# Reordering the end of layer 0 and the last scan step of a four-layer convolution and state-space kernel

## The chip, the cores and the metric

The kernel runs on one core of a Trainium2 chip. The metric is the device time of one execution in microseconds. The kernel before was timed three times: 3322.79, 3324.20 and 3326.24 us, median 3324.2 us. One more execution was profiled; times inside it count from the start of its span.

Names used below: PE is the matrix engine (PEld its weight loads), DVE the vector engine, ACT the scalar engine, POOL the GpSimd engine, SP the engine that only issues transfers. All data are 32-bit floats.

## The reference, cut to what matters

The input x has 3 images of 256 channels and 48 x 48 pixels. Four layers follow one another, each as x = x + layer(group_norm(x)):

- Layer 0: a 1x1 convolution with SiLU gives y1 and y2; y2 passes two blocks of attention and MLP, in which the three images are query, key and value of each other; then y1, y2 and the two block results are concatenated and go through a 1x1 convolution with SiLU.
- Layer 1: a 3x3 convolution whose weights differ by image. Eight experts' weights are mixed with a routing vector made from the image's channel means:

```
pooled = x.mean(axis=(2, 3))
routing = jax.nn.sigmoid(pooled @ routing_ws)
ws = jnp.einsum('ne,eoihw->noihw', routing, weight)
```

- Layer 2: a 3x3 convolution with one set of weights and a bias.
- Layer 3: a state-space layer. Per image it runs a recurrence over 2304 tokens for 512 channels with 16 states each, `hst = hst * dA + dt * B * u`, and reads out `y = sum over states of hst * C`, then gates with silu(z) and projects back to 256 channels.

## The kernel before, in words

The image index b runs in the order ORDER = (2, 1, 0) almost everywhere, and the 2304 pixels are cut into six chunks of 384.

**End of layer 0** (lines 1002 to 1102). For each image two loops of six chunks follow each other. In the first, the MLP of the second block: `hidden` (line 513) makes two products and two gelus, `add_back` (line 526) makes two accumulated products in PSUM tile acc, of which there are three, and DVE adds them to cur[b] (line 533). In the second, `concatenated` (line 1027) multiplies the three stored strips yc of a chunk and the chunk of cur[b] with the last weights (line 1031), ACT applies SiLU (line 1036), and POOL adds the input strip xc (line 1041). DVE then takes statistics of the chunk before (line 1045). The strips yc (576 KB) and xc (384 KB) are loaded by `parts` (line 1017) through ACT's queue; three are requested in front of the loops, and then, in chunk number k, those of chunk k + 2. The pool of the strips has three buffers of each.

After the six chunks of an image the generator `routing` (line 359) is put in line. It makes the group norm of the new image, the channel means and the routing vector. Each call of `aside` (line 1054) advances it to its next yield. Its last piece broadcasts the pooled means on DVE (pbc, line 373, one buffer), multiplies them with the routing weights on PE (line 374), for both halves of the channels, and ends with a sigmoid on ACT (line 378).

**Expert mixing.** `mixed(2, ...)` (line 265) is another generator, for the first image of layer 1. It has 48 steps of one 128x768 piece of an expert's weights (8 experts x 2 channel halves x 3 taps); each piece is loaded by SP into one of six buffers wconv (line 251). The six steps of the first expert run on ACT (line 294), the other 42 on DVE (line 296, an accumulation in u). Two more steps then make `kernel_transform` (line 254), one for each channel half: six DVE operations, lines 258 to 263, from the three mixed taps to six transformed ones, with one wconv buffer for an intermediate. `aside(n)` advances the mixing n steps, from the moment that route[2] exists: 2 in each MLP chunk, 3 in each concatenation chunk.

**Input transform.** Layer 1 is a Winograd-like convolution: `input_transform` (line 316) pads and scales half an image with two ACT operations (line 331) and three POOL fills (lines 322, 325) into the tile xpad, which has one buffer, and makes six transformed inputs vt with twelve DVE operations (lines 345 to 356). For the first half of image 2 it is called in chunk 3 of the last image's concatenation. `products` (line 1623) multiplies vt with u on PE (line 1627); `output` (line 1635) adds the products into x on DVE (lines 1645 to 1657). Five PSUM tiles hold products. While the convolution of image 2 runs, image 1's weights are mixed beside it.

**Order of the work.** `keep_order` (line 2120) chains the instructions of PE, DVE, ACT and POOL, each in the order in which they were written, from a mark to the place of its call. It covers the two loops at the end of layer 0 up to the rest of the mixing (line 1096), and the whole of layer 3 (there with SP too). What is written in between, the routing of image 0 and layers 1 and 2, is not chained; a planner sorts it by its own estimate of when operands are there, and may set such an instruction between two chained ones.

**Last step of layer 3** (lines 2007 to 2115). A step is a chunk, a channel group m and a half h of the states; it has eight scans on DVE (line 1942), one after the other, whose decays ACT makes ahead (line 1934). There are 144 steps; `end` is the last. After a step POOL multiplies its states with C (`times_c`, line 1950), and `add_states` (line 1969) sums the products of the step before over the states: PE multiplies them with a folding matrix into y_ps (line 1964). `keep_busy` (line 1367) issues products that nobody reads, called fillers, into the spare columns of the PSUM tile ps_r (line 1370). In the last step C is copied to that PSUM tile (line 2019) and the products with C are made in three pieces on DVE (`last_product`, line 1983), each followed by its sums. The fillers and the sums stand there so:

```
                n = busy.get((m, h, part), 0)
                if (s == 0 and 2 <= part <= 5) or (s == end and 4 <= part <= 6):
                    n = 3
...
            if s >= 1:
                add_states(s - 1)
```

The fillers of part 4 to 6 are written after `last_product((0,), (2, 3))` of part 5 or around it; the sums of step end - 1 are written after the last scan. Then follow the last sums, the gate (line 1993), four products (line 1407), two copies and the store (lines 1417, 1418).

Of the kernel before, what the change touches and what calls it, by code (L numbers as in the profile page):

```python
# [84 lines left out]
def net(  # L85
# [273 lines left out]
    def routing(b, psum, tag, stats):  # L359

        mv, sc, sh = yield from group_norm_steps(b, psum, tag, stats)
        norms[b] = sixth(sc, sh)
        pooled = small.tile([P, CT], F32, name="pooled")
        nc.vector.tensor_tensor(pooled, mv[:, :, 0], sc, ALU.mult)
        nc.vector.tensor_tensor(pooled, pooled, sh, ALU.add)
        yield
        pr = psum.tile([P, 512], F32, tag=tag, name="ps_r")  # L370
        for ct in range(CT):
            pbc = small.tile([P, P], F32, name="pbc", bufs=1)
            nc.vector.tensor_scalar(pbc, ones, pooled[:, ct : ct + 1], None, ALU.mult)
            nc.tensor.matmul(
                pr[:, :EXPERTS], pbc, rwt[:, ct, :], start=ct == 0, stop=ct == CT - 1
            )
        r = route[b] = const.tile([P, EXPERTS], F32, name=f"route{b}")
        nc.scalar.activation(r, pr[:, :EXPERTS], AF.Sigmoid)


    with ExitStack() as l0:
# [36 lines left out]
        with ExitStack() as p1:  # L418
# [15 lines left out]
            for b in ORDER:  # L434
                xb = xin.tile([P, CT, N], F32, name="xb")

                parts = 6 if b == ORDER[0] else 1
# [576 lines left out]

        def parts(b, c):

            yc = ypool.tile([P, 3, CH], F32, name="yc")
            nc.scalar.dma_start(yc, ycat[b][:, :, c * CH : (c + 1) * CH])  # L1020
            xc = ypool.tile([P, CT, CH], F32, name="xc")
            nc.scalar.dma_start(
                xc, x[b, :, c * CH : (c + 1) * CH].rearrange("(t p) n -> p t n", p=P)
            )
            return yc, xc

        def concatenated(b, c, yc, xc):
            pz = pair()
# [18 lines left out]
        i = NB - 1  # L1047
        mark = listed[-1]
        chunks = [(b, c) for b in ORDER for c in range(NCH)]
        ahead = [parts(*chunks[z]) for z in range(3)]  # L1050
        small_steps = [mlp_weights(i, 0)]
        mixing = mixed(2, upools[0])

# [11 lines left out]
        for n, b in enumerate(ORDER):  # L1065
            held = None
            for c in range(NCH):
                f = hidden(b, c)
                if held is not None:
                    add_back(i, *held)  # L1070
                held = b, c, f
                aside(2)
            add_back(i, *held)
            stats = [
                small.tile([P, NCH, 6], F32, name=f"xst{m}", bufs=2) for m in range(CT)
            ]
            for c in range(NCH):
                concatenated(b, c, *ahead.pop(0))

                z = n * NCH + c + 2  # L1080
                if 3 <= z < len(chunks):
                    ahead.append(parts(*chunks[z]))
                if c:
                    take_stats(b, c - 1, stats)
                if b == 0 and c == 3:
                    vp = late_pool("vp", 2, last_pools)
                    pad = late_pool("pad", stack=last_pools)
                    first_v = input_transform(2, 0, *norms[2])
                aside(3)
            take_stats(b, NCH - 1, stats)  # L1090
            if b:
                curpools[b].close()
            small_steps.append(routing(b, psm, "m", stats))
# [14 lines left out]
    rooms, w3v, chunks, stored = {}, {}, {}, set()  # L1108
# [699 lines left out]
    with ExitStack() as l3:  # L1808
# [198 lines left out]
        for s, (at, m, h) in enumerate(steps):  # L2007
            if m == 0 and h == 1 and at + 2 <= last:
                fetch(at + 2)
            for part in range(8):  # L2010
                j = 4 * m + 2 * h + part // 4
                scan(s, part)
                decay(8 * s + part + 3)
                if s == end and part == 0:
                    c_rows = psr.tile([P, 2, 512], F32, name="ps_r")
                    spread_tiles[:] = [c_rows]
                    tiles["c"], tiles["hc"] = c_rows, hcp.tile([P, 2, 4, CH], F32, name="hc")
                    for g in range(2):
                        nc.tensor.matmul(
                            c_rows[:, g, :CH], ident, chunks[at].bc[1][:, 2 * h + g, :],  # L2020
                            start=True, stop=True,
                        )
                if s == end and part == 3:
                    begin_sums(chunks[at], m)
                    last_product((0, 1), (0, 1))
                if s == end and part == 5:
                    last_product((0,), (2, 3))
                n = busy.get((m, h, part), 0)
                if (s == 0 and 2 <= part <= 5) or (s == end and 4 <= part <= 6):
                    n = 3  # L2030
                if n:
                    g, q = parts_of_step[part]
                    keep_busy(tiles[s][:, g, q, 1 : P + 1], n)
                if s == end and part == 0:
                    for mo in range(2):
                        project_y(chunks[at], mo, 0, 2)
                if s == end and part == 2:
                    gate(at, DI - 2)
                    for mo in range(2):
                        project_y(chunks[at], mo, 2, DI - 1)  # L2040
                if s == end - 1 and part == 0:
                    residual(chunks[at])
                if part == 0 and h == 0:
                    c, n = (at, m + 1) if m + 1 < DI else (at + 1, 0)
                    if c <= last:
                        rows = getattr(chunks[c], "rows", {})
                        chunks[c].rows = {**rows, n: spread(chunks[c], n)}
                if part == 0 and h == 1 and s + 1 < len(steps):
                    spread_second(chunks[steps[s + 1][0]], steps[s + 1][1])
                if part == 4 and s + 1 < len(steps):  # L2050
                    first_states(s + 1)
                if s == 0:
                    if part == 0:
                        scanned = next(
                            i for i in reversed(listed) if i.engine == mybir.EngineType.DVE
                        )
                        tc.add_manual_dep(
                            last_write, scanned.name,
                            mybir.DependencyInfo(
                                mybir.DependencyClass.NoSync, mybir.DependencyReason.DATA  # L2060
                            ),
                            reason="order",
                        )
                    if part == 1:
                        fill_upper(1, 0, 1)
                    if part == 0:
                        run(at, j, PE_)
                    if part in (0, 3, 4, 6):
                        next(pending)
                    if part in (0, 2, 4):  # L2070
                        ct, lo, hi, t = late_copies[part // 2]
                        copy_tokens(ct, lo, hi, t)
                    if part == 5:
                        for copied in last_tokens()[2:]:
                            store_copied(*copied)
                if s == 1:
                    if part % 2 == 0:
                        diagonal(part // 2)
                    if part == 1:
                        next(pending)  # L2080
                if part % 4 == 0:
                    run(at, j, BEGIN)
                if part % 4 == 1:
                    run(at, j, MID)
                if part % 4 == 2:
                    run(at, j, DONE)
                if h == 1 and part == 7 and 3 <= s < end:
                    gate(*steps[s - 3][:2])
                if part % 4 == 3:
                    run(at, j, LATE)  # L2090
                if part == 3 and s:
                    run(at, j, PE_)
            if s + 1 < len(steps):
                fill(s + 1)
            if s == 0:
                next(pending)
            last_states(s)
            if s == end:
                last_product((1,), (2, 3), (2, 3))
            else:  # L2100
                times_c(s)
            run(at, 4 * m + 2 * h + 1, PE_)
            if s >= 1:
                add_states(s - 1)

            if h == 0 and s + 2 < len(steps):
                spread_pe(chunks[steps[s + 2][0]], steps[s + 2][1])
# [122 lines left out]
```

## Time and profile before

| What | us |
|---|---|
| runs: lowest, median, highest | 3322.79, 3324.20, 3326.24 |
| the profiled execution, its own time | 3321.43 |
| its span, first to last instruction | 3319.7 |
| PE busy, DVE busy, ACT busy, POOL busy | 3142.7, 2859.8, 2394.6, 1335.6 |
| DVE scans of layer 3 (L1942), 1152 | 1002.3 |
| PE products of layers 1 and 2 (L1627), 1728 | 429.6 |
| mixing step on DVE (L296), each | 0.95 to 1.01, started 0.93 apart |
| first matmul of the concatenation (L1031), last end | 1350.0 to 1495.6 |
| first product of layer 1 (L1627) | 1514.4 |
| first product of the last output (L1407, after the gate) | 3310.7 |

An instruction is named by its line, engine and tiles (result <- operands). "Idle before" is the time that the engine stood still before it, with the instruction or transfer that ended the wait. Matmul ends are modelled, and one multiplication of 32-bit floats stands as two matmuls in the trace. PEclk or "granted clock" is the share of the full PE clock. A DMA share is the mean busy share of the 16 transfer engines.

### The profile page before, as it was taken

How to read it: one execution, taken by the hardware profiler on the slowest of the kernel's cores; microseconds unless marked ns; L12 is line 12 of the kernel's file. 1: busy time of each engine (PE TensorE's matmuls, PEld its weight loads, DVE VectorE, ACT ScalarE, POOL GpSimd, SP SyncE). 2: the span in 40 equal slices, each digit the busy share in tenths (PEclk: the TensorE clock that was granted, in tenths of full speed). 3: DMA queues.
4: the chain of work that ended last, by engine and by line, in shares of the span. 5: the costliest groups of instructions: out<-in, count | busy, mean ns of one | idle time of the engine just before them, and what ended most of it. 6: DMA issues, size and time to landing. Idle time of an engine off the chain costs nothing.

```text
span 3319.7 us, 54251 instructions
## 1 busy us (share of the span) xinstructions
PE 3142.7 (95%) x20936; PEld 1559.1 (47%) x20936; DVE 2859.8 (86%) x3225; ACT 2394.6 (72%) x3676; POOL 1335.6 (40%) x457
## 2 busy tenths in 40 slices
PE   7999999999999999987999998999999999999996
PEld 4334343353343434555777774444444444444442
DVE  3799989968988998269985449999999999999998
ACT  3688888838888887432324458888888888888884
POOL 0000000000000000120000008999999999999997
PEclk9999999999999999998999999999999999999998
DMA  4000000010000001485621025555555555555652
GB/s 170 30 8 10 8 9 7 8 47 5 8 7 8 9 8 33 148 275 171 212 98 42 34 69 137 137 131 129 133 135 142 138 139 132 122 135 141 147 128 56
DMA packets 182656, 290.98 MB, mean 88 GB/s; under 512 B 34849, under 2 KB 148961, under 8 KB 180466
## 3 DMA queue, kind: packets, MB, share of 16 engines
q1 hardware_dynamic: 169426, 268.53, 30.2%
q10 hardware_dynamic: 12960, 18.88, 1.8%
q8 instruction: 166, 2.72, 0.4%
q14 instruction: 104, 0.85, 0.1%
HBM read 236.24 MB, written 50.64 MB: 86 GB/s over the span
## 4 chain that ended last, share of the span: by engine, by line
PE 54%; DVE 29%; ACT 8%; issue 4%; DMA 2%; POOL 1%; SPq 0%; ACTq 0%; DVEq 0%; POOLq 0%
DVE hs L1942 19%; PE ps_s L638 16%; PE acc L651 14%; PE ps_c L1627 7%; DVE hs L1889 3%; ACT ps_da L1934 2%; DVE u L296 2%; PE ps_y L462 2%; PE ps_s L1031 2%; PE ps_m L665 2%; PE ps_m L711 1%; PE acc L529 1%; PE ps_s L518 1%; PE ps_g L1222 1%; DMA wconv<-in_we 1%
## 5 line engine op out<-in xcount | busy, mean ns | idle before, releaser
L642 ACT ACTIVATE pt<-ps_s 128x1024 f32<-128x1024 f32 x972 | 942.4, 1022 | 154.7 <-PE ps_s L638 142.0
L1942 DVE TENSOR_TENSOR_SCAN hs<-ps_da,hs 128x385 f32<-128x385 f32 x1152 | 1002.3, 934 | 6.1 <-ACT ps_da L1934 5.0
L857 DVE TENSOR_TENSOR part<-part,pt 128x2048 f32<-128x2048 f32 x396 | 906.5, 2289 | 41.3 <-ACT pt L642 18.5
L1934 ACT ACTIVATE ps_da<-dtr,u 128x384 f32<-128x384 f32 x1136 | 642.2, 580 | 116.1 <-DVE hs L1942 105.3
L164 POOL TENSOR_TENSOR rstd<-ve,mhalf 128x2 f32<-128x2 f32 (+1 forms) x25 | 15.7, 628 | 1422.8 <-DVE ve L162 1422.8
L638 PE MATMUL ps_s<-q,kt 32*128 32x512 f32 (+1 forms) x4320 | 576.4, 592 | 0.1
L651 PE MATMUL acc<-pt,vt 128*32 128x512 f32 (+1 forms) x4320 | 520.9, 561 | 0.2
L1627 PE MATMUL ps_c<-vt,u 128*128 128x288 f32 x1728 | 429.6, 409 | 21.9 <-DVE u L263 21.9
L1950 POOL TENSOR_TENSOR hc<-hs,x 128x3072 f32<-128x3072 f32 x72 | 405.5, 5632 | 10.2 <-DVE hs L1942 5.5
L1950 POOL TENSOR_TENSOR hc<-hs,bc 128x3072 f32<-128x3072 f32 x71 | 400.1, 5635 | 8.9 <-DVE hs L1942 4.6
L1627 PEld LDWEIGHTS ps_c<-vt,u 128*128 128x128 f32 x1728 | 328.9, 191 | 117.7 <-issue 20.7
L638 PEld LDWEIGHTS ps_s<-q,kt 32*128 32x128 f32 x4320 | 195.2, 183 | 199.1 <-issue 120.2
L651 PEld LDWEIGHTS acc<-pt,vt 128*32 128x32 f32 x4320 | 94.4, 108 | 353.4 <-issue 326.7
L1964 PE MATMUL ps_y<-hc,u 128*32 128x384 f32 x2304 | 223.8, 505 | 2.1 <-POOL hc L1950 1.1
L1908 POOL TENSOR_TENSOR hs<-dtur,bc 128x1536 f32<-128x1536 f32 x72 | 209.7, 2913 | 0.0
L1273 PE MATMUL ps_g<-u 128*128 128x384 f32 x576 | 195.3, 492 | 11.7 <-ACT u L1269 11.7
L1908 POOL TENSOR_TENSOR hs<-dtur,x 128x1536 f32<-128x1536 f32 x70 | 203.7, 2910 | 0.0
L1273 PEld LDWEIGHTS ps_g<-u 128*128 128x128 f32 x576 | 108.4, 191 | 95.0 <-ACT u L1269 22.5
L1643 ACT COPY cb<-ps_c 128x288 f32<-128x288 f32 x48 | 19.1, 399 | 154.2 <-PE ps_c L1627 129.2
L322 POOL MEMSET xpad<- 128x212 f32 x12 | 5.6, 470 | 307.5 <-ACT xpad L1678 227.7
L1964 PEld LDWEIGHTS ps_y<-hc,u 128*32 128x32 f32 x2304 | 61.6, 111 | 140.3 <-issue 126.8
L1392 PE MATMUL ps_g<-u 128*128 128x384 f32 x288 | 109.2, 513 | 13.1 <-ACT sz L1400 7.7
(295 smaller groups left out, 4163.0 us busy)
## 6 DMA issues: line engine op xcount, KB each, us to landing
wconv<-in_we SPq DMA_DIRECT2D x144, 384.0 KB, 4.3
dtr<-dtd SPq DMA_DIRECT2D x284, 192.0 KB, 3.7
dtur<-dtud SPq DMA_DIRECT2D x284, 96.0 KB, 4.2
wconv<-xd SPq DMA_DIRECT2D x36, 384.0 KB, 4.2
x<-bcd SPq DMA_DIRECT2D x72, 192.0 KB, 4.8
dtd<-x SPq DMA_DIRECT2D x36, 384.0 KB, 3.1
bc<-bcd SPq DMA_DIRECT2D x72, 192.0 KB, 4.9
dtuq<-dtud SPq DMA_DIRECT2D x284, 48.0 KB, 2.0
```

Of the source, the lines that this page charges most:

```text
L638: nc.tensor.matmul(s[:, j, cols], kt[r, mt * P : (mt + 1) * P], q[r, :n], start=True, stop=True,)
L642: nc.scalar.activation(p[:, h0 : h0 + 2, :], s, AF.Exp)
L651: nc.tensor.matmul(acc[h * HD : (h + 1) * HD, :n], vt[:, mt, g * P + h * HD : g * P + (h + 1) * HD], p[:, h, cols], start=mt == 0, stop=mt ...
L857: ): nc.vector.tensor_tensor(part, first, p, ALU.add)
L1273: nc.tensor.matmul(bank[m % 2], w3v["taps"][:, m, tap, :], w3v["xi"][:, m % 3, tap : tap + CH], start=tap == 0, stop=tap == DCONV - 1,)
L1392: nc.tensor.matmul(bank[j], w("in", ct * 512 + m * P, P), k.xn[:, ct, DCONV - 1 :], start=ct == 0, stop=ct == CT - 1,)
L1627: nc.tensor.matmul(pc[:, :HN], u[:, i, dy, ct, m * P : (m + 1) * P], vt[:, i, ct, dy * TW : dy * TW + HN], start=ct == 0 and dy == 0, stop ...
L1908: nc.gpsimd.tensor_tensor(states(s)[:, :, 2:4, 1:], chunks[at].rows[m][1].unsqueeze(1).broadcast_to([P, 2, 2, CH]), b_rows(s, 0, 2), ALU.mult,
L1934: nc.scalar.activation(slots[n % 3][:, 1 : CH + 1], chunks[at].rows[m][0][:, q, :], AF.Exp, scale=amat[:, col : col + 1],)
L1942: nc.vector.tensor_tensor_scan(b, slots[(8 * s + part) % 3][:, : CH + 1], b, 0.0, ALU.mult, ALU.add)
L1950: nc.gpsimd.tensor_tensor(hc, tiles[s][:, :, :, 1:], cb.broadcast_to([P, 2, 4, CH]), ALU.mult)
L1964: nc.tensor.matmul(k.y_ps[32 * q : 32 * q + 32, :CH], fold, hc[:, g, q, :], start=False, stop=g == 1 and q in ends,)
```

## The change

Four edits, all of order; no computation is added or left out except for the fillers.

1. In `routing`, for images 1 and 0 a yield is put between each broadcast on DVE and its product on PE, so that the product is issued an aside later. (For image 0 the generator is run at once, so its order stays.)
2. `parts` is split: xc is still requested two chunks ahead, yc now three chunks ahead, and after xc.
3. In the last image, `aside` advances the mixing three steps instead of two in every second MLP chunk, and in chunk 2 of the concatenation it runs the mixing to its end, both kernel transforms included. This is one chunk ahead of the input transform, which stays in chunk 3.
4. In the last step of layer 3 the fillers of parts 4 to 6 go, and the sums of the step before are issued in part 5, behind `last_product((0,), (2, 3))`, instead of after the last scan.

```diff
@@ routing
             nc.vector.tensor_scalar(pbc, ones, pooled[:, ct : ct + 1], None, ALU.mult)
+            if b < 2:
+                yield
             nc.tensor.matmul(
@@
-        def parts(b, c):
-
+        def rows_of(b, c):
             yc = ypool.tile([P, 3, CH], F32, name="yc")
             nc.scalar.dma_start(yc, ycat[b][:, :, c * CH : (c + 1) * CH])
+            return yc
+
+        def tokens_of(b, c):
             xc = ypool.tile([P, CT, CH], F32, name="xc")
             nc.scalar.dma_start(
                 xc, x[b, :, c * CH : (c + 1) * CH].rearrange("(t p) n -> p t n", p=P)
             )
-            return yc, xc
+            return xc
@@
-        ahead = [parts(*chunks[z]) for z in range(3)]
+        ahead = [(rows_of(*chunks[z]), tokens_of(*chunks[z])) for z in range(3)]
+        rows_ahead, tokens_ahead = ([pair[j] for pair in ahead] for j in range(2))
@@
-                aside(2)
+                aside(3 if n == 2 and c % 2 else 2)
@@
-                concatenated(b, c, *ahead.pop(0))
+                concatenated(b, c, rows_ahead.pop(0), tokens_ahead.pop(0))
 
                 z = n * NCH + c + 2
                 if 3 <= z < len(chunks):
-                    ahead.append(parts(*chunks[z]))
+                    tokens_ahead.append(tokens_of(*chunks[z]))
+                if z + 1 < len(chunks):
+                    rows_ahead.append(rows_of(*chunks[z + 1]))
                 if c:
                     take_stats(b, c - 1, stats)
                 if b == 0 and c == 3:
                     vp = late_pool("vp", 2, last_pools)
                     pad = late_pool("pad", stack=last_pools)
                     first_v = input_transform(2, 0, *norms[2])
-                aside(3)
+                aside(3 if n < 2 or c < 2 else 99)
@@
                 if s == end and part == 5:
                     last_product((0,), (2, 3))
+                    add_states(end - 1)
                 n = busy.get((m, h, part), 0)
-                if (s == 0 and 2 <= part <= 5) or (s == end and 4 <= part <= 6):
+                if s == 0 and 2 <= part <= 5:
                     n = 3
@@
             run(at, 4 * m + 2 * h + 1, PE_)
-            if s >= 1:
+            if 1 <= s < end:
                 add_states(s - 1)
```

## The prediction, made before the changed kernel was run

> **What bounds the kernel now.** I first read the page's engine shares. PE is busy 95% of the span and DVE 86%, so anything that shifts by less than a few microseconds can only be found in stretches where PE stops. I then asked for the busy time in stretches around the two places that the diff touches: the end of layer 0 (1402 to 1600 us) and the last step (3290 to 3320 us).
>
> ```profile
> 1402.00:1440.00 38.00, 34.50 (x101) 19.41 (x100) 21.96 (x29) 9.03 (x14) 9.78 (x6) 0.96 0.91 310
> 1440.00:1464.00 24.00, 19.53 (x54) 10.94 (x55) 16.63 (x35) 11.51 (x17) 2.78 (x2) 0.86 0.71 241
> 1464.00:1496.00 32.00, 30.83 (x95) 17.59 (x93) 18.76 (x23) 9.26 (x13) 10.44 (x8) 1.00 0.74 246
> 1496.00:1514.40 18.40, 0.00 (x0) 0.00 (x0) 18.30 (x23) 7.81 (x10) 2.51 (x4) 0.62 0.19 64
> 1514.40:1600.00 85.60, 83.79 (x331) 62.14 (x331) 81.81 (x143) 17.29 (x27) 1.54 (x4) 0.98 0.64 218
> ```
>
> The columns are the stretch, its length, busy us of PE, PEld, DVE, ACT and POOL, granted clock, DMA share, GB/s. The reader is to see the fourth row: for 18.4 us PE does nothing while DVE never rests. The first two rows show PE short by 3.5 and 4.5 us. In the last row PE and DVE are both full, so neither can start layer 1 late without moving the end.
>
> The timeline then says what PE waits for, and what DVE did meanwhile.
>
> ```profile
> 1414.23 3.47 PE L1031 MATMUL ps_s<-yc,w0b 128*128 128x384 f32 x6 [1.92 <-DMA yc<-ycat]
> 1428.03 2.17 PE L1031 MATMUL ps_s<-yc,w0b 128*128 128x384 f32 x6 [1.54 <-DMA yc<-ycat]
> 1453.17 0.59 PE L374 MATMUL ps_r<-rwt,pbc 128*128 128x8 f32 x2 [3.55 <-DVE pbc L373]
> 1489.94 0.81 DVE L345 SCALAR_TENSOR_TENSOR wc<-xpad 128x624 f32<-128x624 f32 x1 [5.67 <-ACT xpad L331]
> 1491.73 2.25 POOL L1041 TENSOR_TENSOR x<-x,xc 128x768 f32<-128x768 f32 x1 [2.67 <-ACT x L1036]
> 1492.23 2.42 DVE L348 TENSOR_TENSOR vt<-wc,we 128x624 f32<-128x624 f32 x1
> 1513.34 0.95 DVE L263 TENSOR_TENSOR u<-wconv,u 128x768 f32<-128x768 f32 x1
> 1514.43 11.18 PE L1627 MATMUL ps_c<-vt,u 128*128 128x288 f32 x38 [18.89 <-DVE u L263]
> ```
>
> In the brackets stand the idle time and what ended it. PE waits twice for a y strip, once for a routing operand behind mixing steps on DVE, and 18.89 us for the kernel transform. DVE itself sat idle 5.67 us at 1484.3 for the input transform's padded rows, though mixing steps and kernel transforms, all needed by the same first product, lay behind it in the written order.
>
> The last step, same view:
>
> ```profile
> 3303.61 0.94 PE L1370 MATMUL ps_r<-hs,ident 128*128 128x128 f32 x6
> 3304.58 0.95 DVE L1983 TENSOR_TENSOR hc<-hs,ps_r 128x768 f32<-128x768 f32 x1 [4.19 <-PE ps_r L1370]
> 3307.90 2.14 PE L1964 MATMUL ps_y<-hc,u 128*32 128x384 f32 x20
> 3310.09 0.56 DVE L1993 TENSOR_TENSOR sz<-ps_y,sz 128x384 f32<-128x384 f32 x1 [1.13 <-PE ps_y L1964]
> ```
>
> DVE waits 4.19 us for fillers (L1370), because they write the PSUM tile that its product L1983 reads. The 20 sums come after all of it, and the gate L1993 waits for them.
>
> **What the Trainium skill says.** (1) "SBUF — State Buffer", section "Who interferes with whom": a DVE instruction with two SBUF inputs and a GpSimd one that reads SBUF exclude each other; the later one waits for the whole of the earlier. The trace agrees: L348 takes 2.42 us under the POOL add, while its twin L347 takes 0.81, so 1.6 us per collision. (2) "TensorE: Matmul & The Clock Gate", Part 1: an idle window of about 3.4 us halves the clock. Here a 1.92 us stall was enough: six matmuls took 3.47 us against 2.10 elsewhere; after 1.54 us they took 2.17. (3) "DMA: Bandwidth & Descriptors", "Issuing engines are not separate DMA queues": loads of both queues share the 16 engines. The trace agrees in kind: at a DMA share of 0.91 strips land up to 7.9 us after issue, median 4.7.
>
> **The change part by part**, in times of this profile.
>
> *Strips three ahead.* A strip goes out when the silu of a chunk starts; the chunk that needs it starts one chunk, 5.16 us, later. The six chunks of b=1 span 1407.19 to 1438.62, first to last silu, 31.43 us; those of b=2, with no wait, 25.80 us (1355.33 to 1381.13). The loss of 5.6 us is 1.92 + 1.54 of waits plus 1.9 of half clock (the stalled chunk's eight strip and state pairs took 7.1 instead of 5.16). One more chunk of lead makes about 10 us against a landing of at most 7.9: the waits go. The number of loads is unchanged, the order on ACT's queue becomes xc then yc, 0.55 us of issue each, as before. The new load reuses the buffer that this chunk's matmuls read; the silus queued ahead of it have waited for those, so it adds no wait; if it blocked, the next silus would stand behind it and then PE's two PSUM pairs. What is late next: the DMA itself. A chunk needs 576 + 384 + 3x384 KB in 5.16 us, 419 GB/s, while the fullest 3.5 us here moved 393. Lead and six weight buffers should bridge six chunks, not more. I take 5.0 us, bounds 2.5 and 5.6.
>
> *Routing in pieces.* PE's wait of 3.55 us at 1453 and the half clock after it (four matmuls 2.91 us instead of 1.45) go in part: the product now comes a step later, but DVE is also given a third mixing step in three of six asides. DVE in the new order, from bn_aggr at 1443.04: 2, 3, 2 steps (0.93 each) and the small operations as in the trace bring pbc to 1454.05; PE would ask for it at 1452.2, so waits 1.9 us, and 0.5 us for the second. PE starts the concatenation at 1459.4 (1461.1 if the clock drops) instead of 1463.46. Its sigmoid follows the last gelu, which saves one table load of 1.28 us on ACT; ACT waits 5.33 us for PE there, so I count nothing. route[1] comes two steps later; its first reader is at 1504.33.
>
> *Mixing and kernel transforms ahead of the input transform.* DVE finishes its MLP work at 1463.4 and steps 40 to 42 at 1466.2. First silu 1464.9 to 1466.6; statistics follow 3.14 us after (as 1468.83 to 1471.97 now): two rounds of 1.02 + 2.80, spaced by PE's 5.16, put the start of the kernel transforms at about 1478.2. From there DVE is never idle: 12 x 0.87 = 10.4 (start to start of L258 to L263), statistics 1.0, input transform 12 x 0.766 = 9.2, and four POOL adds of chunks 2 to 5, each holding DVE 1.65 us, 6.6. End 1505.4 instead of 1514.3: **8.9 us**. Cover that is lost: adds that met an idle DVE now meet a busy one (four, before two). Bounds: 15.5 with no collision; 4 if the planner, which orders what is not chained, slips about five mixing steps of the next kernel (0.93 each) between the dependent operations. It cannot slip the second half's input transform, as it did before (L345 to L348 stand between L258 and L263), because its padded tile has one buffer. SP's loads keep their number and come as buffers free, some 7 us earlier. After the first product DVE has 11.6 us left of statistics and second transform, before 12.9 (with the second kernel transform), so layer 1 moves whole.
>
> *Last step.* PE runs without a break from 3291.44 to 3303.68. Then: no fillers (0.88 and 1.53 us away), 4 sums 0.65 (L1983 no longer waits, ends 3301.4), 16 sums 4 x 0.33 = 1.3 (their POOL product ended 3300.66), last 4 sums 0.65 (DVE free at 3304.15): 3306.3 instead of 3310.06, **3.7 us**. PE is not idle in it, so the clock should hold; if it drops, 1.2 us are lost. Bounds 2.5 and 4.2. Behind the moved sums on PE stand only the last sums.
>
> Sum: 5.0 + 8.9 + 3.7 = 17.6. The profiled execution took 3321.43 us, 1.7 more than its span of 3319.7; it becomes 3303.8. The median of the runs, 3324.2, lies 2.8 above the profiled one; it becomes **3306.6**.
>
> **Rivals.** (A) Layer 1 keeps the bubble's gain: PE is full from 1532 to 1590 and idles 8 us from 1590 to 1690, where new waits for the second mixing (DMA wconv, up to 2.48 us on DVE) can take it back. Then 5.0 + 3.7 and 1 or 2 remain: 3314. For it: both engines are full. Against: both are ahead by the same. (B) The DMA stays the bound in b=1: 0.91 share already. The strips gain 1 instead of 5: 3310.6. Against: troughs of 0.64 and 0.68 share at the two waits. (C) More: collisions fall in gaps, 12 to 13 in the bubble: 3302. (D) Slower: the free order of layer 1. Its instructions aren't chained; with other ready times the planner may put mixing steps ahead of output additions, so that PE's five product buffers come free late. PE loses some 10 us of the 176 from 1514 to 1690 now; it decides against the change once that loss passes 10 + 17.6 + 6.7 = 34 us, a fifth of the stretch: 3332. That the change does nothing is excluded for the last step, whose wait is written in the code.
>
> **Numbers.** Forecast 0.58, A 0.18, B 0.10, C 0.08, D 0.04, no change 0.02. A measurement of this kernel tells about 0.2% (6.6 us) from no change. Faster: forecast, B, C and most of A, 0.88; same: A's weak end and the last, 0.08; slower 0.04. The likeliest case alone reaches from 3302 to 3311; with A's centre, B and C the range is 3301 to 3315.
>
> **What would show it.** Right: silus of b=1 25.8 us apart first to last; no wait for yc; kernel transforms before L345; PE idle about 15 us before the first product; no wait of L1983 for L1370. Wrong: yc waits at a DMA share near 1; mixing steps between L258 and L356; more PE idle before 1690 than now; half clock at the gate.

## The result, and the profile after

| | runs | lowest, median, highest us | ratio to before, 95% |
|---|---|---|---|
| before | 4 | 3322.79, 3323.69, 3326.24 | |
| changed | 4 | 3301.28, 3303.97, 3306.90 | 0.9939 [0.9927, 0.9951] |
| changed, once more, later | 5 | 3301.98, 3304.69, 3308.43 | 0.9942 [0.9928, 0.9955] |

The change gains 19.7 us in the first comparison and 18.8 in the second (3323.45 before); the forecast was 17.6, the predicted time 3306.6. The profiled execution of the changed kernel took 3306.9 us, span 3305.1; it is the slowest of its four, 3.1 us above the 3303.8 that the prediction gave for the profiled execution.

Two runs of the same code differ by several us before the changed places begin (the first SiLU of the concatenation falls anywhere from 1352.2 to 1359.0 us in the profiles of this study), and layer 3 varies by 2.4 us. So I measure four stretches inside each profile. Silu k is the first SiLU (L1036 before, L1040 after) of chunk k, counted over the three images.

| stretch, us | before (range with three kernels like it up to there) | changed, two profiles | gain; of A to C on the mean of the four |
|---|---|---|---|
| A: silu 6 to 11, image 1's chunks | 31.44 (30.8 to 32.2) | 25.80, 25.80 | 5.6 |
| B: silu 11 to 12, the last image's MLP | 30.20 (29.1 to 30.3) | 29.52, 26.78 | 0.4 and 3.1 |
| C: silu 12 to the last product of layer 2 | 537.2 (537.2 to 539.4) | 530.7, 532.2 | 7.7 and 6.3 |
| D: scan 1145, the last step's first, to the gate | 17.23 (17.0 to 18.0, other kernels with the old last step) | 12.39, 12.95 | 4.8 and 4.3 on before |

A to C together: a mean of 599.8 us in the four kernels (598.9 to 600.7), 586.1 and 584.8 in the two profiles: 14.4 us gained on the mean of the two (forecast 5.0 + 8.9 = 13.9). With D it makes some 19.

The busy time in stretches of the changed kernel, columns as before: stretch, length, PE, PEld, DVE, ACT, POOL, clock, DMA share, GB/s.

```profile
1404.00:1436.40 32.40, 32.37 (x102) 18.76 (x100) 24.02 (x28) 9.08 (x14) 10.39 (x6) 1.00 0.95 330
1436.40:1459.20 22.80, 18.48 (x53) 10.58 (x54) 19.04 (x35) 9.48 (x16) 2.74 (x2) 0.85 0.87 305
1459.20:1490.60 31.40, 31.29 (x97) 17.96 (x95) 27.79 (x29) 9.48 (x13) 12.54 (x8) 1.00 0.79 278
1490.60:1498.10 7.50, 0.08 (x2) 0.04 (x1) 7.39 (x9) 5.47 (x7) 1.80 (x1) 0.83 0.31 100
1498.10:1584.60 86.50, 85.08 (x332) 62.89 (x332) 82.65 (x147) 19.96 (x32) 2.59 (x7) 0.98 0.54 189
1584.60:1591.80 7.20, 0.01 (x1) 0.01 (x1) 7.17 (x10) 7.20 (x11) 0.69 (x3) 0.71 0.51 198
```

First row: in image 1's concatenation PE is now never idle, at a DMA share of 0.95. Second: in the MLP that follows it still lacks 4.3 us. Fourth: the empty stretch ahead of layer 1 is 7.5 us long, not 18.4. Last row: a new one, 7.2 us without PE at the change to layer 1's second image, DVE full in it.

PE's timeline of the changed kernel names what it waited for.

```profile
1441.93 2.93 PE L531 MATMUL acc<-f,w0b 128*128 128x384 f32 x4 [4.05 <-ACT f L525]
1457.58 0.39 PE L376 MATMUL ps_r<-rwt,pbc 128*128 128x8 f32 x2 [0.26 <-DVE pbc L373]
1498.09 11.05 PE L1634 MATMUL ps_c<-vt,u 128*128 128x288 f32 x36 [7.42 <-ACT u L294]
1591.79 20.72 PE L1634 MATMUL ps_c<-vt,u 128*128 128x288 f32 x72 [7.20 <-DVE u L263]
```

No wait for a strip is left in this profile (the second has one, 0.66 us in the last image); the routing operand costs 0.26 us in place of 3.55 and 0.38; the first product waits 7.42. Against that stand 4.05 us for a gelu, with half clock behind it (four matmuls in 2.93 us, elsewhere 1.45), and 7.20 us at the second image. The releaser "ACT u L294" was long done; DVE's timeline shows what came last:

```profile
1477.91 2.45 DVE L259 SCALAR_TENSOR_TENSOR u<-u,wconv 128x768 f32<-128x768 f32 x1
1482.25 2.46 DVE L262 TENSOR_TENSOR u<-wconv,u 128x768 f32<-128x768 f32 x1
1487.49 2.56 DVE L260 SCALAR_TENSOR_TENSOR u<-u,wconv 128x768 f32<-128x768 f32 x1
1492.07 2.55 DVE L263 TENSOR_TENSOR u<-wconv,u 128x768 f32<-128x768 f32 x1
1497.02 0.81 DVE L347 TENSOR_TENSOR vt<-wc,we 128x624 f32<-128x624 f32 x1
1503.99 0.81 DVE L356 SCALAR_TENSOR_TENSOR vt<-we,vt 128x624 f32<-128x624 f32 x1
```

Four of the twelve transform steps take 2.45 to 2.56 us instead of 0.96, each beside a POOL addition. The first product started at 1498.09, just behind L347 (end 1497.83), and six microseconds ahead of L356. It needs one of the six transformed inputs, not all. DVE itself came less far forward: its first operation on the products (L1645 before, L1652 after) starts 58.7 us after silu 12 in the kernel before, 53.8 and 53.0 in the changed one. PE's first product gained 12 to 13 us (45.61 to 33.53 and 32.60), DVE 4.9 and 5.7.

The last step, PE first, then DVE:

```profile
3293.82 2.81 PE L1971 MATMUL ps_y<-hc,u 128*32 128x384 f32 x32
```

```profile
3291.89 0.95 DVE L1990 TENSOR_TENSOR hc<-hs,ps_r 128x768 f32<-128x768 f32 x1
3294.59 0.95 DVE L1990 TENSOR_TENSOR hc<-hs,ps_r 128x768 f32<-128x768 f32 x1
3296.70 0.56 DVE L2000 TENSOR_TENSOR sz<-ps_y,sz 128x384 f32<-128x384 f32 x1 [1.16 <-PE ps_y L1971]
```

The products with C (L1990) follow the scans without a wait (before: 4.19 and 0.75 us), and all 32 matmuls of the sums run in one row of 2.81 us.

### The profile page after: what moved, and what is told of

It is laid out like the page before. It is cut to its first block, busy times and chain, and to the rows that moved or that the text cites. A ratio compares the mean times of both kernels' runs of the same rounds, so it can differ in the third digit from the quotient of the medians.

```text
span 3305.1 us, 54212 instructions
## 1 busy us (share of the span) xinstructions
PE 3140.9 (95%) x20918; PEld 1557.1 (47%) x20918; DVE 2867.9 (87%) x3225; ACT 2393.1 (72%) x3675; POOL 1338.7 (41%) x457
## 4 chain that ended last, share of the span: by engine, by line
PE 55%; DVE 28%; ACT 8%; issue 5%; DMA 2%; POOL 1%; SPq 0%; DVEq 0%; ACTq 0%; POOLq 0%
DVE hs L1949 19%; PE ps_s L640 16%; PE acc L653 15%; PE ps_c L1634 8%; DVE hs L1896 3%; ACT ps_da L1941 2%; PE ps_s L1035 2%; PE ps_y L464 2%; DVE u L296 2%; PE ps_m L667 2%; PE ps_m L713 1%; PE acc L531 1%; PE ps_g L1229 1%; PE ps_s L520 1%; DMA wconv<-in_we 1%
## 5 line engine op out<-in xcount | busy, mean ns | idle before, releaser
L859 DVE TENSOR_TENSOR part<-part,pt 128x2048 f32<-128x2048 f32 x396 | 906.7, 2290 | 41.2 <-ACT pt L644 18.4
L1634 PE MATMUL ps_c<-vt,u 128*128 128x288 f32 x1728 | 431.9, 410 | 17.6 <-DVE u L263 9.0
```

What stands on the lines that cost most here:

```text
L859: ): nc.vector.tensor_tensor(part, first, p, ALU.add)
L1634: nc.tensor.matmul(pc[:, :HN], u[:, i, dy, ct, m * P : (m + 1) * P], vt[:, i, ct, dy * TW : dy * TW + HN], start=ct == 0 and dy == 0, stop ...
```

## The experiments

In the expectations "layer 2" stands in several places for layer 1 (its kernel transforms, its first product, its first unit, its change of image); "the end of layer 2" is the last product of both convolutions. Ratios are to the kernel before, in runs beside it.

| run | median us | ratio, 95% | A | B | C | D |
|---|---|---|---|---|---|---|
| e1_tail_only | 3318.35 | 0.9985 [0.9979, 0.9992] | 30.83 | 30.28 | 538.0 | 12.17 |
| e2_no_fillers_only | 3318.64 | 0.9985 [0.9977, 0.9992] | 31.35 | 29.90 | 539.3 | 12.24 |
| e2b_move_only | 3324.88 | 1.0003 [0.9995, 1.0012] | 32.15 | 29.14 | 539.4 | 18.21 |
| e3_strips_only | 3315.97 | 0.9978 [0.9968, 0.9988] | 25.80 | 31.86 | 537.6 | 18.02 |
| e4_mixing_only | 3318.78 | 0.9986 [0.9979, 0.9992] | 31.45 | 30.60 | 533.8 | 17.04 |
| e5_no_split_routing | 3308.48 | 0.9960 [0.9946, 0.9974] | 25.80 | 30.71 | 530.6 | 12.18 |
| e6_late_loads | 3302.40 | 0.9935 [0.9921, 0.9948] | 25.80 | 27.57 | 530.9 | 12.18 |
| e7_short_adds | 3299.92 | 0.9931 [0.9917, 0.9944] | 26.08 | 26.34 | 524.0 | 12.18 |
| e8_less_mixing | 3298.28 | 0.9929 [0.9916, 0.9943] | 25.80 | 27.44 | 527.2 | 12.18 |
| e9_dve_adds | 3301.69 | 0.9934 [0.9921, 0.9948] | 25.80 | 26.61 | 528.9 | 12.29 |
| e10_dve_adds_late | 3300.08 | 0.9927 [0.9913, 0.9940] | 25.80 | 26.59 | 526.3 | 12.35 |

**The last step: e1, e2, e2b.** The kernel before with both halves of edit 4 (e1), without fillers only (e2), with the sums moved only (e2b).

```diff
@@ e1 and e2b
+                    add_states(end - 1)
...
-            if s >= 1:
+            if 1 <= s < end:
@@ e1 and e2
-                if (s == 0 and 2 <= part <= 5) or (s == end and 4 <= part <= 6):
+                if s == 0 and 2 <= part <= 5:
```

Expected of e1:

> The kernel before with the last part of the change alone: no fillers in the last step, and the sums of the last but one step moved into its part 5. Each theory is read from the stretch between the scan number 1144 (the last step's first) and the gate's end, inside one profile. Mine: this part owes nothing to the other two, so the stretch is 4.9 us shorter than in the kernel before (17.2 us from that scan to the gate's start there, 12.4 us after the whole change), the median is 3323.7 - 4.9 = 3318.8 us, and nothing ahead of the last step moves by more than 0.5 us. Rival, the parts help each other (the last step comes in a better state because the stages ahead end sooner): less than 3 us here, 3321 us or more.

Expected of e2:

> The kernel before without the fillers of the last step's parts 4 to 6, the sums left where they were. Mine: the fillers stand in TensorE's queue between the last products, so they cost their own duration, but the last sums still come one behind the other after the last scans: the stretch from scan 1144 to the gate is shorter by 1.5 to 3.5 us, median 3320.2 to 3322.2 us. Rival, the sums' place alone makes the gain: under 0.5 us here. Second rival, the fillers alone make it: 4.5 us or more here.

Expected of e2b:

> The kernel before with only the sums of the last but one step moved into part 5 of the last, the fillers kept. Mine: since the run without fillers and without moved sums had the whole gain, the moved sums alone shorten the stretch from scan 1144 to the gate (17.2 us in the kernel before) by no more than 1.5 us, as the last product still waits for the fillers. Rival, either of the two is enough: 4 us or more.

e1 gains 5.1 us in D and 4.8 in the median, so the last step owes the other edits nothing. But e2 has the whole of it, 5.0 us, and my share for the fillers (1.5 to 3.5) was wrong: the second rival holds. The last step of e2, PE and then DVE:

```profile
3307.20 2.81 PE L1964 MATMUL ps_y<-hc,u 128*32 128x384 f32 x32
```

```profile
3308.13 0.95 DVE L1983 TENSOR_TENSOR hc<-hs,ps_r 128x768 f32<-128x768 f32 x1
3310.09 0.56 DVE L1993 TENSOR_TENSOR sz<-ps_y,sz 128x384 f32<-128x384 f32 x1 [1.00 <-PE ps_y L1964]
```

With the sums left at their old place the 32 matmuls still take 2.81 us in one row, and the gate follows the last product at the same distance (1.96 us from start to start; 2.11 in the changed kernel). DVE's scans and products set the end in both, and the sums fit in front of it. With the move alone (e2b), DVE:

```profile
3306.86 0.95 DVE L1983 TENSOR_TENSOR hc<-hs,ps_r 128x768 f32<-128x768 f32 x1 [4.06 <-PE ps_r L1370]
3311.57 0.95 DVE L1983 TENSOR_TENSOR hc<-hs,ps_r 128x768 f32<-128x768 f32 x1 [2.04 <-PE ps_r L1370]
```

The second wait for fillers grows from 0.75 to 2.04 us, since the moved sums now stand in front of them on PE. D is 18.21, at or above the top of the kernels with the old order (17.0 to 18.0): no gain, if anything 0.2 to 1.2 us lost.

**Strips and mixing apart: e3, e4.** The kernel before with edit 2 alone, and with edit 3 alone.

```diff
@@ e3
+                    tokens_ahead.append(tokens_of(*chunks[z]))
+                if z + 1 < len(chunks):
+                    rows_ahead.append(rows_of(*chunks[z + 1]))
@@ e4
-                aside(2)
+                aside(3 if n == 2 and c % 2 else 2)
-                aside(3)
+                aside(3 if n < 2 or c < 2 else 99)
```

Expected of e3:

> The kernel before with the y strips loaded three ahead and nothing else. Mine: the concatenated matmuls of image 1 wait no more for yc, the six chunks take 25.8 us instead of 31.4, and of these 5.6 us what reaches the first product of layer 2 is what is left once ScalarE issues its loads late before the next MLP: 5.0 to 6.3 us at the last silu of image 2, and the same at the end since nothing behind it is changed: 3317.4 to 3318.7 us. Rival, the transfers are the bound (they only crowd earlier): the chunks gain but the MLP behind them gives back 4 us or more, and the end is at 3321.5 us or later. Second rival, layer 2 gives it back at its change of image as in the whole change: end gain under 3 us.

Expected of e4:

> The kernel before with the counts of the mixing steps alone (all of image 0's mixing and the kernel transforms of layer 2 in front of its input transform). Mine: the first product comes about 12 us earlier, each of the four transforms takes some 1.6 us longer where it meets an addition of GpSimd, and at the change to image 1 TensorE waits for VectorE's kernel transform, so that the end is only 6 to 8 us earlier: 3315.7 to 3317.7 us. Rival, it is the whole bubble: the end is 11 us or more earlier, and no wait over 3 us stands at the change to image 1. Second rival, the four collisions eat it: under 3 us.

In e3, A gains 5.6 us as in the whole change, B gives back 1.7 (31.86 after 30.20), C gains 0.9 on the four kernels' mean of 538.5: A to C is 595.2 against a mean of 599.8, 4.6 us. The first rival (the transfers give back 4 us or more) and the second (under 3 us at the end) don't hold. My own 5.0 to 6.3 us at the end was a little high. The median is 7.2 us lower, below my 3317.4 to 3318.7, with an interval that reaches from 4 to 11.

In e4 the first product comes 12.0 us earlier after silu 12 (33.57 instead of 45.61), as expected, but only two of the four collisions fell into the kernel transforms and two into the input transform, and A to C is 595.9: 3.9 us, less than my 6 to 8. The wait for the kernel transform at the change to image 1 is there, 6.17 us. PE in the last image's chunks of e4, and its first product:

```profile
1479.44 3.62 PE L1031 MATMUL ps_s<-yc,w0b 128*128 128x384 f32 x6 [2.73 <-DMA yc<-ycat]
1493.23 2.17 PE L1031 MATMUL ps_s<-yc,w0b 128*128 128x384 f32 x6 [1.78 <-DMA yc<-ycat]
1505.16 8.48 PE L1627 MATMUL ps_c<-vt,u 128*128 128x288 f32 x34 [1.37 <-ACT x L1036]
```

The four kernels with the old counts have one wait of 0.72 to 1.78 us where the first of the two stands, and none over 0.3 us behind it. The strips issued from 1463 to 1500 us land after a median of 6.8 us, at most 7.7, in e4, and after 4.5 and 5.6 in the kernel before; two chunks of lead no longer cover that. That the faster mixing's weight pieces cause it is shown in part only. SP issues 4 of them from 8 to 22 us after silu 12, where the kernel before has 1, and this fits the second wait. In the 8 us on either side of silu 12 it issues 9 instead of 10, so the number of pieces does not explain that the first wait is longer.

Silu 12 to 17 takes 32.2 us in e4, 26.8 to 28.3 in the four kernels, 26.2 and 26.7 in the changed kernel. Little of these 5 us counts: the first product of e4 comes as soon after silu 12 as that of the changed kernel (33.57; 33.53 and 32.60), since DVE sets most of that time in both. L347, which the product needs, ends 31.8 us after silu 12 in e4 and 33.3 in the changed kernel; the late chunks then hold the product for 1.37 us more. At the end of layer 2, C is 1.6 and 3.1 us longer than in the changed kernel.

Edits 2 and 3 are worth 4.6 and 3.9 us alone. Together, without the edit of the routing (e5 below, A to C 587.1), they bring 12.7 us. So the two edits help each other by some 4 us, about half of it in B and half in C, where one code alone varies by 1 to 3 us. That the third chunk of lead keeps the last image's strips on time may be the reason for the part in C; this is not shown. No term of the prediction had it.

**Routing in one piece, late loads, and the changed kernel once more: e5, e6.** The changed kernel without the yields of `routing`; and with the loads behind an image's last chunk issued in MLP chunk 2 of the next.

```diff
@@ e5
-            if b < 2:
-                yield
@@ e6
+                if n and c == 2:
+                    load_ahead(n * NCH + 1)
...
+                if c < NCH - 1:
+                    load_ahead(z)
```

Expected of e5:

> The changed kernel with the routing in one piece again, as before. Mine: VectorE's third mixing step stands in front of the routing operand, TensorE waits some 4.5 us for it (as in the run with the mixing alone: 4.47 us) and runs at half clock behind it, so silu 12 (the first of the last image) comes 3 to 5 us later than in the changed kernel; the first product comes later by about as much, and the end of layer 2 by 1 to 4 us: median 3305 to 3308 us. Rival, the prediction's: ScalarE waits there for TensorE anyway and nothing is gained by the pieces: silu 12 within 1 us of the changed kernel, the end too.

Expected of e6:

> The changed kernel, with the loads that stand behind the last chunk of an image on ScalarE's queue issued two chunks of the next MLP later. Mine: what holds TensorE 4.05 us at 1441.93 us for ScalarE's gelu is ScalarE standing in the issue of two loads behind full DMA queues; without them that wait falls under 1.5 us, no half clock follows it, silu 12 comes 3 to 5 us earlier (counted from silu 11) and the first product 2 to 5 us earlier; how much reaches the end of layer 2 depends on VectorE: 0 to 3 us, median 3301 to 3304 us. Rival, the wait is that of the table load behind the last silu and not of the queue: silu 12 within 1 us. Second rival, the strips now land late for the last image: waits for yc of 2 us or more there, and the end later than in the changed kernel.

Expected of after_again:

> The changed kernel itself once more, for the spread of its own stretches: mine, the stretch from silu 11 to silu 12 (29.53 us in its first profile) is 26 to 28 us here, as in two of the kernels that differ from it only behind that place, since what ScalarE's loads wait for behind full DMA queues varies; the stretch from the first product to the end of layer 2 is within 1 us of the first profile's 497.2 us. Rival: 29.5 us again, so that the late loads gained 2 us.

In e5 the waits are back, PE's timeline:

```profile
1447.63 0.39 PE L374 MATMUL ps_r<-rwt,pbc 128*128 128x8 f32 x2 [3.32 <-DVE pbc L373]
1448.40 0.39 PE L374 MATMUL ps_r<-rwt,pbc 128*128 128x8 f32 x2 [0.38 <-DVE pbc L373]
```

B is 30.71, the longest of the kernels with edits 2 and 3 together (26.3 to 29.5), but only 1.2 us above one profile of the changed kernel, and A to C is 587.1, 1.0 and 2.3 us above the two. So the pieces take away the waits for the operand, but what of that reaches the end is not shown: 1.0 and 2.3 us are no more than the 1.8 us by which the four kernels with one code differ, and the medians' intervals overlap. Nor are my 3 to 5 us at silu 12 (1.2 and 3.9).

The gelu's wait is explained by ACT's timeline in the changed kernel:

```profile
1437.87 0.37 ACTq L1026 DMA_DIRECT2D xc<-in_x  x1
1439.37 0.53 ACTq L1021 DMA_DIRECT2D yc<-ycat  x1
1440.00 1.28 ACT L525 ACT_TABLE_LOAD   x1 [3.74 <-DMA wconv<-in_we]
1441.30 2.00 ACT L525 ACTIVATE f<-ps_s,fb 128x384 f32<-128x384 f32 x4
```

ACT's last SiLU ended at 1436.26, but its two loads went out at 1437.87 and 1439.37, and the table load and gelus stand behind them. The releaser named, a weight piece of SP, is the true one. The chain that led to the gelu, followed back from it, begins:

```profile
1431.54 7.81 DMA wconv<-in_we
1439.35 0.02 issue
```

In the trace each load names a semaphore, a counter that its landing raises, and ACT's two issues wait for the very semaphores that they then use again. The transfer that had used it before was a weight piece each time: issued by SP at 1430.61 and 1431.53, landed 7.2 and 7.8 us later, at 1437.79 and 1439.35; ACT's issues followed after 0.08 and 0.02 us. In the changed kernel 7 of the 12 strip and token loads of image 1's chunks go out within 0.08 us of such a landing; in the kernel before none does (0.38 us at the nearest). The buffers had been free before (the addition of chunk 10 ended at 1433.2), so ACT was held by transfers of another queue that landed late. With the loads later, e6's PE:

```profile
1436.94 1.56 PE L531 MATMUL acc<-f,w0b 128*128 128x384 f32 x4 [0.41 <-ACT f L525]
1439.27 0.38 PE L186 MATMUL ps_gm<-mv,gmat 128*128 128x2 f32 x2 [0.77 <-DVE mv L183]
1449.79 0.49 PE L376 MATMUL ps_r<-rwt,pbc 128*128 128x8 f32 x2 [1.90 <-DVE pbc L373]
```

The wait goes from 4.05 to 0.41, so it was the two loads that held the gelu (0.41 in e10 too). Yet B, 27.57, lies between the two profiles of the changed kernel (29.52 and 26.78): PE then waits for DVE's statistics and routing operand instead. In after_again the same wait was 2.30 us, and B 26.78, within the 26 to 28 that I expected. What I took for a loss of 4 us was one draw of a varying wait, and DVE's operands come little before its end. My expectation that C's part behind the first product would repeat within 1 us fell as well: 497.2, then 499.6.

**Who bounds layer 1's first image: e7, e8.** The changed kernel with POOL's additions on chunks 2 to 5 of the last image cut to 4 columns per half (e7), and with five mixing steps of image 1's last expert as copies of 8 columns on ACT (e8).

```diff
@@ e7
+            if b == 0 and c >= 2:
+                nc.gpsimd.tensor_tensor(both[:, :, :4], both[:, :, :4], xc[:, :, :4], ALU.add)
@@ e8
+                    elif b == 1 and e == EXPERTS - 1:
+                        nc.scalar.copy(dst[:, 0, :8], wt[:, 0, :8])
```

Expected of e7:

> The changed kernel with GpSimd's addition of the tokens on chunks 2 to 5 of the last image cut to 4 columns per half; so most of that image's residual is left out there. Mine: each addition holds VectorE 1.6 us in four kernel transform steps; without them the transforms take 12 x 0.96 us, the first product comes 5.5 to 7 us earlier, and as VectorE is the engine that layer 1's first unit waits for, at least 4 us of it are left at the end of layer 2: median 3298 to 3300 us. Rival, TensorE bounds the first unit: under 2 us at the end of layer 2.

Expected of e8:

> The changed kernel with five of the mixing steps of image 1's last expert turned from VectorE steps of 0.93 us into copies of 8 columns on ScalarE; those parts of that expert are left out. Nothing ahead of the first product changes. Mine: VectorE bounds the first unit of layer 2, TensorE's wait of 7.20 us for image 1's kernel transform falls to 2 to 4 us, and the end of layer 2 comes 3 to 4.7 us earlier (5 x 0.93): median 3299 to 3301 us. Rival, TensorE bounds it and the 7.20 us are only slack that it builds up: end within 1 us of the changed kernel.

e7: all twelve transform steps take 0.95 or 0.96 us, the first product comes 27.94 us after silu 12 instead of 33.53 and 32.60, and C falls by 6.7 and 8.2 us to 524.0: DVE's 6.4 us (4 x 1.6) reach the end in full. In e8 nothing changes ahead of the first product, and at the change of image PE shows

```profile
1573.07 2.74 PE L282 MATMUL ps_g<-wconv,each 128*128 128x384 f32 x8
1576.29 0.38 PE L186 MATMUL ps_gm<-mv,gmat 128*128 128x2 f32 x2 [0.48 <-ACT xpad L1680]
1576.82 13.36 PE L1636 MATMUL ps_c<-vt,u 128*128 128x288 f32 x54
```

The wait of 7.20 us is gone (I expected 2 to 4 left), and C is 3.5 and 5.0 us shorter, for 4.65 us taken from DVE. So DVE bounds this part, and PE's rival falls: PE's early start only fills its wait at 1591.

**Can it be better: e9, e10.** The changed kernel with the additions of the last image's chunks 3 to 5 on DVE in front of their statistics; e10 with e6's late loads too.

```diff
@@ take_stats
+            if b == 0 and c in later:
+                both, xc = later.pop(c)
+                nc.vector.tensor_tensor(both, both, xc, ALU.add)
```

Expected of e9:

> The changed kernel with the additions of chunks 3, 4 and 5 of the last image made by VectorE, in front of the statistics of the chunk, instead of by GpSimd. Mine: three of four collisions in the kernel transforms go (3 x 1.6 us) and three additions of 0.96 us come behind the input transform, so the first product comes 4 to 5 us earlier (counted from silu 12), and the end of layer 2 is earlier by the 1.9 us that VectorE has less: median 1 to 3 us under the changed kernel of this call. Rival, what TensorE gains ahead is lost at the change to image 1 in full: no gain at the end of layer 2.

Expected of e10:

> The run before with the last chunk's loads issued two chunks of the next MLP later as well. Mine: the 2 us of the late loads (ahead of silu 12) and the 1.9 us of the additions add up: median 2 to 5 us under the changed kernel of this call. Rival: the late loads' gain was the spread between runs of one code (that stretch differed by 3 us between runs in which nothing ahead of it was changed) and nothing is added.

DVE in e9: one collision is left (the additions on DVE come behind the input transform, the first at 1494.95).

```profile
1472.87 2.44 DVE L259 SCALAR_TENSOR_TENSOR u<-u,wconv 128x768 f32<-128x768 f32 x1
```

In e9 the first product comes 28.80 us after silu 12, 3.8 and 4.7 us earlier, and C is 1.9 and 3.3 us shorter, as expected from 3 x (1.6 - 0.96). The medians are 3301.69 and 3300.08, 3.0 and 4.6 us under the changed kernel measured beside them (3304.69), but the intervals of the ratios overlap. B is the same in both (26.61 and 26.59), so the late loads add nothing there and the rival holds; what e10 has more is in C, where the code is the same. e10 is the fastest full version measured, not one shown to be faster than the changed kernel.

## Why the prediction was right, step by step

*Strips three ahead, 5.0 us:* right, 5.6 in A in both profiles and in e3 (least in e7, 5.4). The landing times that I put against the 10 us of lead were not those of this stretch: 4.7 and 7.9 us are the median and the most of all 18 strips, while at the share of 0.91 they were 6.5 and 6.8. In image 1's stretch the changed kernel's strips took a median of 8.1 us and up to 9.0 (9.9 in its second profile). The lead was just enough. "It adds no wait" was wrong: I looked at the buffers, and the new loads wait for the semaphores of earlier transfers. That a load which blocks holds the silus behind it was said; what it held was the table load and the gelu of the next MLP. I gave it no price; it took 2.3 to 4.05 us of PE's time in the kernels with edits 2 and 3 that issue these loads at the image's end, and little of the end (e6).

*Routing in pieces:* it has no term of its own in the sum, but the 8.9 us of the next term start from a first silu at 1464.9 to 1466.6, which is 2.2 to 3.9 us ahead of the 1468.83 of the kernel before, and the pieces were to bring that. B gained 0.4 and 3.1. The waits of 1.9 and 0.5 us are what the runs show where no load holds the gelu (1.90 in e6; 1.90 and 0.44 in e10). In the changed kernel they were 0.26 and 0.43 us, because PE had stood 4.05 and 2.30 us for the gelu before, while DVE went on. It is luck that the one loss, which I had not priced, hid much of the other.

*Mixing ahead, 8.9 us:* right in B and C together, 8.1 and 9.4 us in the two profiles. Right too: four collisions of 1.6 us (the Trainium skill, "SBUF — State Buffer", section "Who interferes with whom"; 2.45 to 2.56 instead of 0.96 us, and none in e7), kernel transforms ahead of L345, and DVE without idle from their start. L356 ends 40.2 and 39.3 us after silu 12; the prediction's 1505.4 is 38.8 to 40.5 us after its own. Wrong: "end 1505.4" as the time of the first product. It waits for L347 and not for L356; the idle ahead of it was 7.4 us, not about 15. That extra start gained nothing, and the forecast had not counted on it: "layer 1 moves whole" held for DVE (4.9 and 5.7 us), while PE, 12 to 13 us earlier, gave the rest back, most of it in one wait of 7.20 us (rival A's shape, with DVE's own work behind it and not a DMA). Missing: SP's earlier loads, which I named ("some 7 us earlier") and set at nothing, and that edits 2 and 3 help each other; e3 and e4 together bring only 8.5 of the 12.7 us.

*Last step, 3.7 us, bounds 2.5 and 4.2:* too low; 4.8 and 4.3 in the two profiles, 5.1 in e1. The failed term is the 24 matmuls at 2.6 us behind the first eight. All 32 took 2.81 us where the first eight alone had taken 1.48, so the others add 1.3. The products are 32 columns wide; that narrow products at different column positions overlap is what the Trainium skill says ("TensorE: Matmul & The Clock Gate", Part 3), and this row agrees: four of its matmuls start within 0.04 us, the next four some 0.32 us later. And I credited the edit as a whole: the fillers are all of it, and the move is worth nothing (e2, e2b).

*Rivals.* B (transfers still the bound in image 1) fell: 25.80 us at a share of 0.95. D (layer 1's free order) did not happen: C is shorter in both profiles. C (more than forecast), 3302, lay as near to the median as the forecast did, but not by its reason: no collision fell into a gap.

*The total.* The profiled execution was put at 3303.8 and took 3306.9; the median was put at 3306.6 and is 3304.0. Four executions of the changed kernel spread over 5.6 us, so a hit within 3 us proves little by itself; the stretches do, and there the last step and A were each 0.6 to 1.1 us better than said.

What stays open: how much of B belongs to the routing and how much to the transfers, since B varies by 3 us in one code; why the first late strip of e4 lands later than before; and what moves layer 3 by 2.4 us between runs.

## What to carry to other kernels

When work is moved ahead so that an engine starts sooner, ask which engine bounds the stretch behind it: only what that engine gains (here DVE's idle time less its collisions) reaches the end, and the rest comes back as a wait further on. Two edits that share the transfer engines must be costed together: here the two brought 8.5 us apart and 12.7 together. A load that a computing engine issues can hold that engine, so ask which earlier transfer the issue waits for. And work that only keeps an engine busy should not write the tile that the critical step reads.

## What had not been expected of the hardware

A load issued by ACT can wait for a transfer that another engine issued: at a DMA share of 0.95 two issues of 0.37 and 0.53 us waited for the landing of two weight pieces of SP, 7.2 and 7.8 us after those had been issued, and held the next ACT instruction for 3.74 us. A wait of 2.34 us (e8) or 3.50 (e3) was followed by half clock (2.86 and 2.93 us for four matmuls), one of 2.78 (e5) was not (1.56): the length of the wait alone does not decide it.
